# The convolution of a decoder kernel: root and scaling in one piece on VectorE, squares summed on ScalarE

## The chip, the cores and the metric

The kernel runs on one core of one Trainium2 chip. The core has five engines with a queue of instructions each: TensorE (PE in the profile, its weight loads PEld), VectorE (DVE), ScalarE (ACT), GpSimd (POOL) and SyncE (SP, which only issues transfers here). The metric is the device time of one execution in microseconds (us), lower is better; a kernel is run several times and the median counts.

## The reference

A decoder with four blocks of three layers (attention, cross attention, feed-forward), each followed by a residual and a layer norm, on 128 sequences of 64 tokens with 128 features, all in fp32. The change lies in the feed-forward of block L2, a convolution with a small mixture of experts, here cut to what matters:

```python
def _L2_ffn_ref(x, ...):                      # x: 128 x 64 x 128
    xc = conv over the last 3 tokens, each feature by itself + dw_bias
    xc = silu(xc @ pw_w.T + pw_b)
    x1 = x + xc
    logits = x1 @ router_w.T + router_b                      # 8 experts
    top_v, top_i = lax.top_k(logits, 2)
    rw = weights of the two best experts (softmax), zero elsewhere
    ye = silu(einsum('bsd,eod->bseo', x1, expert_w) + expert_b)   # all 8 experts
    combined = einsum('bse,bseo->bso', rw, ye)
    moe_out = combined @ out_w.T + out_b
    a = x1 + moe_out
    h = norm_w * (a / sqrt(mean(a * a) + 1e-6))              # the RMS norm
    ff = gelu(h @ ff_down_w.T + ff_down_b)                   # 128 -> 32
    return h + ff @ ff_up_w.T + ff_up_b
x = layernorm(x + _L2_ffn_ref(x, ...))
```

## The kernel before

The 8192 tokens stay in SBUF as 16 chunks of 512 tokens (`X[c]`, 128 partitions x 4 tiles x 128 features). The convolution, `conv_steps` (L1907 to L2113), takes them in pairs: `turns` is 8, and `pair` is the two chunks of a turn. The work of a turn is written as three parts.

- `begin(i)` (L1943 to L1981) is a generator that prepares turn i: the transposes of X (L1949), the three matmuls of the convolution (L1960), its SiLU on ScalarE (L1962), the sum x1 on GpSimd (L1963), the router's logits (L1968 to L1974) and `top2` on VectorE (L1976, then the helper's L428 to L475, with one tanh on ScalarE, L470). Its result is the table of expert weights `s["w"]`.
- `units(i, n, t)` (L1985 to L2000), eight of them per turn, is the expert work of 128 tokens: matmuls into two PSUM banks (L1992, biases L1994), two SiLU of 512 columns on ScalarE (L1996), the product with the expert weights on VectorE (L1997, 1024 columns), and the sum over the eight experts, its first step on VectorE for even t and on GpSimd for odd t (L1998), the others on GpSimd (L1999, L2000). The units write into a ring of four buffers, and their matmuls into a pool of five PSUM banks.
- `end(i)` (L2002 to L2056) is a generator that finishes turn i: transposes of the experts' sum (L2007) and copies (L2008); the output matmuls (L2016, L2017); on VectorE the biased sum `acc` (L2019); its square on ScalarE (L2021) and the reduction on VectorE (L2022); then the roots; the scaling by root and `norm_w` in eight steps on VectorE (L2033); transposes of the result (L332, copies L339), the residual on GpSimd (L2039, L401), the down and up matmuls (L2044, L2052) with a Gelu between (L2046), and the residual sum (L2054).

`norm` (L2058 to L2067) takes one reciprocal square root for two things at once: the mean squares of turn i and the variances of the layer norm of turn i - 1, whose statistics `ln_stats` computes (L373 to L376). `rsqrt` (L342 to L353) is eleven small dependent instructions on VectorE, on 128 x 16 values: a seed by bit operations (L347, L348) and three Newton steps (L350, L351, L352). `ln_apply` (L379) then writes the layer norm to `X` with a small VectorE step (L382) and four ScalarE instructions per chunk (L385).

The loop at L2083 to L2106 interleaves the three: while the units of turn i are issued one by one, `take` advances the generators of turn i + 1 (`b`), turn i - 1 (`e`) and what is left of turn i - 2 (`tail`). So the order in which the program is traced is set by hand:

```python
elif g == 3:
    take(e, 3)        # acc and squares of both chunks, then norm
elif g == 4:
    take(e)           # the scaling, L2033
...
elif g == 7:
    take(e, 2)        # the transposes of the scaled rows
```

That traced order gives the priority; a scheduler at compile time places each engine's instructions, and takes a later one first where the earlier isn't ready in its model. The order within an engine's queue is fixed after that. `tc.issue_after(ins)` adds an edge: each instruction traced in the block on the engine of `ins` comes behind `ins` in that queue. Before the change no such edge stands inside the loop.

## Time and profile before

| | |
|---|---|
| median of 3 runs | 3176.83 us (3161.66 to 3185.31) |
| profiled execution, own time | 3181.66 us |
| its span | 3179.6 us |
| mean granted TensorE clock | 0.934 |
| busy over the span | PE 88%, PEld 65%, DVE 64%, ACT 51%, POOL 48% |
| expert matmuls of the convolution (L1992) | first at 2125.6 us, last at 2431.2 us |
| one turn of the convolution | 42.2 us from the first L1960 to that of the next turn |
| busy in such a turn | PE 38.5, DVE 35.2, POOL 25.8, ACT 20.9 us |

The profile is one execution as the hardware profiler recorded it. A line of a timeline has the start in us from the span's start, the duration, the engine, the line of the kernel, the operation, the tile written and the tiles read with their shapes, and how many such instructions it merges; in brackets stands the idle time before, with what ended it. A line of the waits has the waiting engine, tile and line, then what it waited for, then the total in us, the number of times and the longest.

### The profile page before, as it was taken

What the parts mean: (1) busy time and instruction counts of PE and PEld (TensorE: products, weight loads), DVE (VectorE), ACT (ScalarE), POOL (GpSimd) and SP (SyncE); (2) the same over time, 40 slices, a digit from 0 to 9 for tenths busy, and PEclk for the clock granted to TensorE, in tenths of its full rate; (3) what the DMA queues carried; (4) which work ended last, traced back from release to release, by engine and by line L of the source; (5) the groups of instructions that cost most, each with busy time, mean ns of one, the idle gap of its engine ahead of it and who ended that gap; (6) DMA issues with size and microseconds to landing.
All of it is one profiled execution on the core that took longest, in us unless ns stands there. A gap on an engine that the chain in (4) does not pass through costs nothing.

```text
span 3179.6 us, 110559 instructions
## 1 busy us (share of the span) xinstructions
PE 2803.0 (88%) x46690; PEld 2051.2 (65%) x46690; DVE 2028.4 (64%) x7310; ACT 1620.5 (51%) x3150; POOL 1516.0 (48%) x1521
## 2 busy tenths in 40 slices
PE   5899979999898899998899989999997679998993
PEld 3789856666666677865577767764433347766882
DVE  3742469667777666553477656667888876674355
ACT  3444468754444465422466555544454556654453
POOL 3566566134555344325277345556665213444244
PEclk9999989999999899889799999989998889997997
DMA  4578921000001100003611000000000000011784
GB/s 128 150 201 261 257 54 43 11 1 3 3 3 44 31 4 4 6 20 98 178 19 18 4 6 4 4 12 1 1 1 7 1 11 18 17 33 49 212 256 120
DMA packets 191633, 182.22 MB, mean 57 GB/s; under 512 B 30176, under 2 KB 166624, under 8 KB 191136
## 3 DMA queue, kind: packets, MB, share of 16 engines
q1 hardware_dynamic: 160688, 136.66, 14.9%
q0 software_dynamic: 20224, 32.28, 4.4%
q8 instruction: 366, 6.00, 0.8%
q10 hardware_dynamic: 10224, 6.22, 0.7%
q14 instruction: 131, 1.07, 0.1%
HBM read 132.34 MB, written 42.73 MB: 55 GB/s over the span
## 4 chain that ended last, share of the span: by engine, by line
PE 55%; DVE 25%; ACT 5%; issue 5%; POOL 5%; DMA 4%; SPq 0%; POOLq 0%; ACTq 0%; DVEq 0%
PE av_ps L1310 9%; DVE m L1243 7%; PE s_ps L1235 6%; PE h_ps L790 5%; PE yg L803 5%; PE t_ps L1273 4%; DMA got<-l_rout,fat 2%; PE ye_ps L1992 2%; PE v_ps L1212 2%; PE xT_ps L332 2%; PE t_ps L1285 2%; POOL x L387 2%; PE y L1134 1%; PE y L1689 1%; DVE lnst L373 1%
## 5 line engine op out<-in xcount | busy, mean ns | idle before, releaser
L1243 DVE TENSOR_REDUCE m<-s_ps 128x8 f32<-128x512 f32 x640 | 397.5, 683 | 122.8 <-PE s_ps L1472 45.4
L1292 ACT ACTIVATE e<-t_ps 128x512 f32<-128x512 f32 x640 | 329.9, 602 | 147.1 <-PE t_ps L1285 146.5
L1310 PE MATMUL av_ps<-vx,e 128*64 128x18 f32 (+1 forms) x10240 | 343.1, 217 | 10.0 <-issue 7.6
L1310 PEld LDWEIGHTS av_ps<-vx,e 128*64 128x64 f32 x10240 | 325.0, 141 | 30.3 <-issue 23.5
L792 ACT ACTIVATE hT<-h_ps,aux 128x256 f32<-128x256 f32 x496 | 206.5, 469 | 218.0 <-PE h_ps L790 105.1
L1273 PE MATMUL t_ps<-eb,kT 32*64 32x128 f32 x10240 | 281.0, 286 | 6.8 <-DVE m L1243 2.4
L1187 POOL TENSOR_SCALAR eb<-qT,small 128x512 f32<-128x512 f32 x75 | 124.1, 1655 | 332.6 <-ACT qT L972 171.2
L825 POOL DMA_INDIRECT got<-l_rout,fat x192 | 193.1, 1006 | 168.0 <-DVE r L835 59.3
L790 PE MATMUL h_ps<-ebT,rw 128*128 128x256 f32 x992 | 241.3, 387 | 13.6 <-DVE ebT L778 8.5
L1273 PEld LDWEIGHTS t_ps<-eb,kT 32*64 32x64 f32 x10240 | 197.9, 132 | 74.0 <-DVE m L1243 25.1
L803 PEld LDWEIGHTS yg<-rw,hT 128*128 128x128 f32 x1984 | 240.7, 192 | 6.3
L803 PE MATMUL yg<-rw,hT 128*128 128x128 f32 x1984 | 241.2, 275 | 0.0
L387 POOL TENSOR_SCALAR x<-xb,lnmv,ln_y 128x128 f32<-128x128 f32 x200 | 157.5, 799 | 169.2 <-DVE ln_y L352 169.1
L1235 PE MATMUL s_ps<-eb,qT 32*64 32x256 f32 x5120 | 220.9, 399 | 10.9 <-DVE m L1243 4.5
L1315 DVE RECIPROCAL rc<-av_ps 128x32 f32<-128x32 f32 (+1 forms) x192 | 61.6, 321 | 241.9 <-PE av_ps L1310 241.8
L765 POOL DMA_INDIRECT aux<-in_x_dram,rat x156 | 160.1, 1026 | 116.3 <-PE h_ps L790 49.1
L790 PEld LDWEIGHTS h_ps<-ebT,rw 128*128 128x128 f32 x992 | 182.0, 194 | 38.4 <-DVE ebT L778 12.9
L804 DVE TENSOR_TENSOR yo<-yg,aux 128x256 f32<-128x256 f32 x124 | 52.3, 422 | 233.4 <-PE yg L803 233.3
L1185 ACT ACTIVATE eb<-qT,small 128x512 f32<-128x512 f32 x160 | 106.9, 715 | 123.6 <-POOL qT L1413 118.9
L1235 PEld LDWEIGHTS s_ps<-eb,qT 32*64 32x64 f32 x5120 | 114.2, 134 | 55.7 <-issue 11.5
L1187 POOL TENSOR_SCALAR eb<-kT,small 128x512 f32<-128x512 f32 x75 | 136.0, 1814 | 24.5 <-ACT kT L972 15.9
L1992 PE MATMUL ye_ps<-w_l2f,box 128*128 128x512 f32 x256 | 135.6, 649 | 0.0
(519 smaller groups left out, 6368.5 us busy)
## 6 DMA issues: line engine op xcount, KB each, us to landing
rw<-in_l0w_dram SPq DMA_DIRECT2D x78, 512.0 KB
rw<-in_l3w_dram SPq DMA_DIRECT2D x46, 512.0 KB
l_rout<-yo SPq DMA_DIRECT2D x124, 128.0 KB
aux<-xd SPq DMA_DIRECT2D x46, 128.0 KB
aux<-in_l0b_dram SPq DMA_DIRECT2D x78, 66.0 KB
xd<-vx SPq DMA_DIRECT2D x5, 1024.0 KB
plan<-xr ACTq DMA_DIRECT2D x18, 256.0 KB
x<-in_x_dram SPq DMA_DIRECT2D x16, 256.0 KB
```

What stands on the lines that cost most here:

```text
L387: (V if on_dve else G).tensor_scalar(X[c][:, t, :], r[:, t, :], mv[:, t, 0:1], y[:, t : t + 1], ALU.subtract, ALU.mult)
L790: s.pe = mm(ps[:, j * GR : (j + 1) * GR], w1[:, (k + j) * P : (k + j + 1) * P], ebT, start=True, stop=True)
L792: s.act_ins = A.activation(hT[k + j], ps[:, j * GR : (j + 1) * GR], s.act, bias=v[:, k + j : k + j + 1])
L803: s.pe = mm(y[:, i * P : (i + 1) * P], hT[k][:, i * P : (i + 1) * P], w2[:, k, :], start=(k == 0), stop=(k == FK - 1))
L825: s.gather = G.indirect_dma_start(out=got[i][k][:, t, :], out_offset=None, in_=s.rout[b][:, :], in_offset=bass.IndirectOffsetOnAxis(ap=at[ ...
L1187: ins = (G if h == 2 and not early else V).tensor_scalar(dst, x, mine, None, ALU.mult)
L1235: mm(ps[g][j * S : (j + 1) * S, u * 256 : (u + 1) * 256].rearrange("p (h k) -> p h k", h=4), rows32(s["q"], g)[:, b], rows32(s["eb"], g)[: ...
L1243: last = V.tensor_reduce(s["m"][:, g, 2 * hf : 2 * hf + 2, :].rearrange("p t h -> p (t h)"), ps[g].rearrange("p (n k) -> p n k", k=S), AX. ...
L1273: mm(ps[g][i * S : (i + 1) * S].rearrange("p (a u j q) -> p a u j q", u=2, a=2, j=2)[:, :, u, j, :], rows32(s["k"], g)[:, b], rows32(s["eb ...
L1292: last = A.activation(e[:, g, :], ps[g], AF.Exp, scale=scale)
L1310: mm(av[j * S : (j + 1) * S, 8 * (u - u0) + n, :], ev[:, n // 2, n % 2, u, j, :], vx[:, 2 * (2 * hf + u) + j, n, :], start=True, stop=True,)
L1992: mm(ps[k].rearrange("p (e d) -> p e d", e=4), s["x1T"][n][:, t * P : (t + 1) * P], w[0][:, 4 * k : 4 * k + 4, :], start=True, stop=False, ...
```

## The change

The root and the scaling of `end(i)` become one step of the generator, right behind the second chunk's sum, and are traced at the slot of unit 3. Each unit traced after that slot, until the next turn's scaling takes its place, is issued with `tc.issue_after(scaled)`, where `scaled` is the last scaling instruction of the turn before; so on VectorE its product and its sum come behind the whole root and scaling. The layer norm's small step and its ScalarE instructions are traced behind the scaling instead of ahead of it. `ln_stats` of a chunk is traced with the sum of that chunk. The slot of unit 4 takes nothing any more; all steps with matmuls keep their slots. The square of a chunk, one ScalarE instruction of 512 columns and a VectorE reduction, becomes four ScalarE instructions of 128 columns that also write their sum (`accum_out`).

```diff
             v = sm.tile([P, 2, 2, TPC], F32, tag="cv", name="cv")
-            acc = []
+            acc, mv = [], []
             for n in pair:
                 ...
                 V.tensor_tensor(h, z.rearrange("p (t d) -> p t d", t=TPC), row("outb")[:, None, :].to_broadcast([P, TPC, D]), ALU.add)
                 sq_ = work("ye", (P, TPC, D), "sq")
-                A.activation(sq_, h, AF.Square)
-                V.tensor_reduce(v[:, 0, n], sq_, AX.X, ALU.add)
+                for t in range(TPC):
+                    A.activation(sq_[:, t, :], h[:, t, :], AF.Square, accum_out=v[:, 0, n, t : t + 1])
                 acc.append(h)
+                if i:
+                    mv.append(ln_stats(S_[i - 1]["r"][n], v[:, 1, n]))
                 yield
             V.tensor_scalar(v[:, 0], v[:, 0], 1.0 / D, 1e-6, ALU.mult, ALU.add)
-
-            y = norm(v, i - 1, S_[i - 1] if i else None)
-            yield
-            hT, base = [], []
+            if not i:
+                G.memset(v[:, 1], 1.0)
+            y = roots(v)
             for n in pair:
                 h = acc[n]
                 for t in range(TPC):
-                    V.scalar_tensor_tensor(h[:, t, :], h[:, t, :], y[:, 0, n, t : t + 1], row("normw"), ALU.mult, ALU.mult)
+                    last = V.scalar_tensor_tensor(h[:, t, :], h[:, t, :], y[:, 0, n, t : t + 1], row("normw"), ALU.mult, ALU.mult)
+            s["scaled"] = last.ins
+            if i:
+                applied(i - 1, mv, y)
             yield
+            hT, base = [], []
             for n in pair:
                 h = acc[n]
                 hT.append(transposed(h, "oT"))
...
-        def norm(v, i, s):
-            ...
+        def roots(v):
+            return rsqrt(v.rearrange("p a n t -> p (a n t)"), 4 * TPC, "rms").rearrange("p (a n t) -> p a n t", a=2, n=2)
+
+        def applied(i, mv, y):
+            for n in pair:
+                ln_apply(2 * i + n, S_[i]["r"][n], mv[n], y[:, 1, n], on_act=True)
...
-        tail = none
+        tail, scaled = none, None
         for i in range(turns):
             ...
             for g in range(8):
-                units(i, g // TPC, g % TPC)
+                with tc.issue_after(scaled) if scaled else nullcontext():
+                    units(i, g // TPC, g % TPC)
                 ...
                 elif g == 3:
                     take(e, 3)
-                elif g == 4:
-                    take(e)
+                    scaled = S_[i - 1]["scaled"] if i else None
                 elif g == 5:
                     take(b)
...
         G.memset(v[:, 0], 1.0)
-        norm(v, turns - 1, S_[turns - 1])
+        mv = [ln_stats(S_[turns - 1]["r"][n], v[:, 1, n]) for n in pair]
+        applied(turns - 1, mv, roots(v))
```

More of the change, by code (lines that the diff above doesn't have):

```diff
@@ L2056, in end @@
             yield
-        def norm(v, i, s):
-            if s is None:
-                G.memset(v[:, 1], 1.0)
-            else:
-                mv = [ln_stats(s["r"][n], v[:, 1, n]) for n in pair]
-            y = rsqrt(v.rearrange("p a n t -> p (a n t)"), 4 * TPC, "rms").rearrange("p (a n t) -> p a n t", a=2, n=2)
-            if s is not None:
-                for n in pair:
-                    ln_apply(2 * i + n, s["r"][n], mv[n], y[:, 1, n], on_act=True)
-            return y
+        def roots(v):
[3 more added lines that the diff above has]
+                ln_apply(2 * i + n, S_[i]["r"][n], mv[n], y[:, 1, n], on_act=True)
         def take(it, n=1):
```

## Prediction

> **What bounds the kernel now.** I began with the page. One execution spans 3179.6 us, its own time is 3181.66 us (2.06 us lie around the span), and the median of the three runs is 3176.83 us, 4.83 us below that execution. The sum below is made on that execution and then shifted by those 4.83 us.
>
> ```profile
> PE 2803.0 (88%) x46690; PEld 2051.2 (65%) x46690; DVE 2028.4 (64%) x7310; ACT 1620.5 (51%) x3150; POOL 1516.0 (48%) x1521
> ```
>
> These shares mix twelve layers. By the source view of L1992 the convolution's expert matmuls run from 2125.6 to 2431.2 us, so whatever the change does must be found in about 355 us, 11% of the span. Inside, the turns repeat: the first L1960 starts at 2250.66, 2292.83, 2335.01 and 2377.17, a period of 42.17 us. The table by stretches for three turns (columns: PE, PEld, DVE, ACT, POOL busy, granted clock, DMA share, GB/s):
>
> ```profile
> 2250.66:2292.83 42.17, 38.95 (x144) 17.68 (x145) 35.24 (x77) 20.85 (x40) 25.85 (x28) 0.92 0.00 1
> 2292.83:2335.01 42.18, 38.54 (x145) 17.27 (x145) 35.20 (x77) 20.86 (x40) 25.84 (x28) 0.92 0.00 0
> 2335.01:2377.17 42.16, 38.53 (x144) 17.53 (x144) 35.24 (x77) 20.85 (x40) 25.84 (x28) 0.92 0.00 1
> ```
>
> PE is nearly full and moves no data to speak of. The view of waits over the same three turns says what PE lacks:
>
> ```profile
> PEld oT_ps L332 <- DVE acc L2033: 15.5, 15, 2.9
> PE oT_ps L332 <- DVE acc L2033: 9.1, 8, 2.1
> PEld u L2052 <- ACT g L2046: 1.7, 2, 1.0
> ```
>
> So one wait matters: the transposes of the scaled rows wait for the scaling. Why that is late is in VectorE's timeline:
>
> ```profile
> 2308.41 0.74 DVE L2025 TENSOR_SCALAR cv<-cv 128x8 f32<-128x8 f32 x1
> 2309.18 0.17 DVE L347 TENSOR_SCALAR rms_b<-cv 128x16 int32<-128x16 int32 x1
> 2309.27 1.22 DVE L1997 TENSOR_TENSOR units<-units,route 128x1024 f32<-128x1024 f32 x1
> ...
> 2312.30 1.24 DVE L351 SCALAR_TENSOR_TENSOR rms_u<-rms_u,cv 128x16 f32<-128x16 f32 x1
> ...
> 2318.66 4.40 DVE L2033 SCALAR_TENSOR_TENSOR acc<-acc,rms_y,rows 128x128 f32<-128x128 f32 x8
> 2322.98 0.21 DVE L436 TENSOR_TENSOR route<-route,t_k 128x64 f32<-128x64 f32 x1
> ```
>
> The root's dozen tiny steps take from 2308.41 to 2317.92, 9.5 us, because products (L1997), sums (L1998) and router steps stand between them.
>
> **Part 1, the root unbroken.** The same steps stand unbroken in the last `end`, where no unit is left: L2025 at 2462.86, the last L352 ending at 2465.34, 2.5 us, then L2033:
>
> ```profile
> 2465.16 0.18 DVE L352 SCALAR_TENSOR_TENSOR rms_y<-rms_u,rms_y 128x16 f32<-128x16 f32 x1
> 2465.52 3.23 DVE L2033 SCALAR_TENSOR_TENSOR acc<-acc,rms_y,rows 128x128 f32<-128x128 f32 x8
> ```
>
> The scaling would end at about 2308.4 + 2.5 + 3.2 to 4.4 = 2314.1 to 2315.3 instead of 2323.1, some 8 us earlier. What PE can take of it: the last L1992 ahead of the transposes ends at 2316.99, the next starts at 2323.12, 6.13 us later; in between lie seven transposes of 0.13 (eight undisturbed ones of L1949 take 1.02) and two L1994 of 0.32, 1.5 us. **4.6 us per turn** is the most that can come back, in six turns (transposes at 2193, 2235, 2277, 2319, 2361 and 2403).
>
> **Part 2, what is late next.** The edges add no instruction; they put the products of units 4 to 7 (4 x 1.14 from start to start) and two sums (2 x 0.60) behind the scaling. Queued behind them on VectorE are the router's steps L1976 to L475; POOL's sums L1998 to L2000 wait for the products, and on POOL's in-order queue L2039 and L401 may stand behind those sums. The chain of waits already shows the router as the next link:
>
> ```profile
> 2281.01 1.14 DVE units L1997
> 2282.15 1.22 DVE route L465
> 2283.37 0.02 issue
> 2283.39 0.23 DVE t_m L428
> 2283.63 0.02 issue
> 2283.65 0.93 DVE route L432
> 2284.58 1.17 DVE t2d L468
> ```
>
> It goes on through the tanh, the SiLU of the next turn's first unit, the table load and the Gelu to L2052 at 2289.01 and L1960 at 2292.83. In the turn of 2292.83, L2052 starts at 2332.00 and the Gelu had ended at 2331.13: only 0.9 us of slack. So what counts is when L468 ends: at 2327.92 now, 19.5 us after L2025 began. After the change the same instructions lie there. Without stalls: root 2.5, scaling 3.2, L382 0.2, products 4.6, sums 1.2, ten router steps at about 0.2 make 13.7 us. To this come waits for POOL. L351 above took 1.24 us instead of 0.17; it ends at 2313.54, and POOL's L1998, which started at 2311.78 for 1.73, ends at 2313.51. Such stretched steps (L351, L350, L352, L382, L2033, L465, L432, L468) add up to about 8 us in this stretch, while POOL ran 11 us. After the change POOL has nothing to sum until the products come, and its 9.9 us (three units' sums 4.8, two L2039 2.6, two L401 2.5) fall on the rest: 4 us of stalls if half hits, 8 us if most does. L468 then ends 17.7 to 21.7 us after L2025, between 1.8 earlier and 2.2 later than now.
>
> So per turn the gain lies between 4.6 (if the SiLU and the Gelu no longer stand behind the tanh on ACT) and -1.3 (if they do and POOL hits: 2.2 less the slack of 0.9). I take **1.0 us**, nearest to the row of the chain: the slack of 0.9 is what PE can win before it meets the second chain, whose own shift I put at nothing. 6 x 1.0 = 6 us.
>
> A row and a rule weighed: the stretched L351 above is one collision. The Trainium skill, "SBUF — State Buffer", section "Who interferes with whom", goes further: every VectorE instruction with two SBUF inputs contends with a GpSimd instruction that reads SBUF, for its whole length. By that rule a turn's POOL work without waits (4 x 1.27 + 8 x 0.73 + 8 x 0.46 + 2 x 1.18 + 2 x 1.31 + 2 x 1.26 = 22.1) and VectorE's two-input work (8 x 1.14 + 4 x 0.60 + 8 x 0.34 + 11 x 0.17 + some 2.2 = 18.3) fill 40.4 of the 42.17 us, an estimate that would cap the gain at 1.8 per turn, 11 us in all, and speaks against the change.
>
> **Part 3, squares on ACT.** Two L2021 (0.63) and two L2022 (0.69) become eight ACT squares of 128 columns with a sum. The page has no such sum. From below: L1827, 128x128, 0.275 each, four make 1.1; from above: L385 at 0.48 each and as much again for the sum, 3.8. Against 0.63 + 0.69 = 1.32 on the path of the second block that is -0.2 to +2.5. I take L385's spacing, 3.19 / 8 = 0.40, four make 1.6: **+0.3 us** per turn, six turns 1.8. VectorE sheds 1.38 us per turn, but in a place where it waits (1.18 and 0.70 us ahead of L2022), so I cost that at nothing; without that cover it would be worth 1.4.
>
> **Part 4, moved steps.** The statistics (L373 to L376) are traced earlier; they ran at 2293 to 2299 already, long before the root: nothing, and 2.8 us if the residual came late. L382 and ACT's eight L385 (3.19 us) go behind the scaling; the oT copies L339 queue behind them, about 2318.5, still before 2321.79 of now: nothing, or 3.2 us if ACT were late. No DMA is touched, and no step of PE, SP or POOL changes its slot.
>
> **Part 5, the last turn.** Here PE stands 6.84 us before the transposes of 2438.94, but VectorE is packed (38.71 us of the 40 from 2400 to 2440), and the second L2007 at 2454.40 waits 4.10 for L2054, which stands behind the next layer's roots. Between 6.84 and a loss of 2.5 I take **4 us**.
>
> **Sum.** -6 + 1.8 - 4 = -8.2 us: 3173.5 on the execution's own time, **3168.6 us** beside the median. I forecast no change that can be told: 1% is about what a measurement of this kernel can tell (31.8 us: below 3145.1 or above 3208.6).
>
> **Rivals.** (A) The forecast, 50%: VectorE with POOL takes over; 3168.6, its own range 3155 to 3185. (B) 20%: PE becomes the only bound, ACT serves the SiLU and the Gelu ahead of the tanh: 6 x 4.6 + 6.84 - 1.8 = 32.6 us, 3144.2. For it: PE's other waits are small; against it: products, router and POOL's sums must still go through VectorE, and 35.2 of 42.17 us are already taken there. (C) 25%, slower: the products held back make POOL's sums and the router late, every tiny router step meets a POOL sum, and PE waits at L2052 and L1992 for ACT behind the tanh: 2.2 from L468 and 2.5 from the squares' upper end, less the slack of 0.9, make 3.8 per turn, six turns and 2.5 at the end: +25, 3202, with 3190 to 3220 around it. It decides once squares and L468 together come more than 0.9 us later than now. For it: the slack of 0.9; against it: VectorE has 2.36 and 0.9 us idle per turn ahead of L1997 and L2054 to absorb it. (D) 5%: the scheduler fills the root's gaps with router steps, and the order of the rest stays: 3176.8.
>
> **How the numbers follow.** Faster by over 1% is half of B (0.10) and a little of A: 0.12. Slower by over 1% is four tenths of C (0.10) and a little of A: 0.12. The rest, 0.76, is within. The low end takes both full gains and the squares' lower end, 27.6 + 6.84 + 1.2 = 35.6 us, 3141, rounded to 3140; the high end, 3206, holds a little over half of C, so that some 2 in 10 lie outside.
>
> **What would show it.** Right: no L1997 between L2025 and the last L2033, which then take 6 to 7.5 us instead of 14.6; the wait at L332 for L2033 falls from 15.5 us in three turns to under 5; the period falls by 0 to 2.5 us; waits at L2052 or L1992 for ACT grow, and L468 ends some 19 us after L2025. Wrong: a period under 39.5 us (B), or over 43.5 (C), or squares above 0.6 us each.

## The result and the profile after

The changed kernel is slower, by a little: a median of 3182.13 us (3166.71 to 3194.1, 20 runs) against 3168.38 us (3149.09 to 3191.43, 20 runs) for the kernel before on the same chip. The ratio is 1.0045, 95% interval 1.0027 to 1.0063. That is far below the 1% of the prediction, and with 20 runs each it is still told from no change: 13.8 us slower, where 8.2 us faster was forecast.

The profiled execution spans 3168.5 us, less than the 3179.6 of before. Single executions scatter by 0.6 to 0.7% to either side, and in these two the stretch ahead of the convolution, which is the same in both programs, differs by 18 us (the first L1992 starts at 2107.7 and at 2125.6). So the traces are compared stage by stage. From the first L1992 to the first instruction of the next layer's scan, the convolution takes 354.7 us before and 362.9 after, 8.2 us more; a second trace of the kernel before, taken later, gives 354.9. The interval of the difference of the medians reaches down to 8.6 us. What the convolution doesn't hold of it, I could not place.

The line numbers after: squares L2022 (L2021 before), mean L2027 (L2025), scaling L2034 (L2033), residual on GpSimd L2044 (L2039), down matmuls L2049 (L2044), Gelu L2051 (L2046), up matmuls "u" L2057 (L2052), residual sum L2059 (L2054). Other steps go by their tiles: oT the transposes of the scaled rows (L332), xT those of X (L1949), sT those of the experts' sum (L2007), pw the convolution's matmuls (L1960), z the output matmuls (L2016, L2017). First the page's line of busy time, then three turns of the changed kernel by stretches, with the same columns as before:

```profile
PE 2768.4 (87%) x46690; PEld 2035.0 (64%) x46690; DVE 2011.8 (63%) x7294; ACT 1630.8 (51%) x3262; POOL 1520.6 (48%) x1521
```

```profile
2234.45:2278.48 44.03, 38.16 (x146) 18.94 (x144) 33.76 (x78) 22.21 (x53) 27.34 (x29) 0.88 0.00 1
2278.48:2322.67 44.19, 38.33 (x146) 18.93 (x144) 33.71 (x74) 22.22 (x53) 26.31 (x29) 0.88 0.00 1
2322.67:2366.91 44.24, 38.39 (x146) 18.93 (x144) 33.55 (x74) 22.21 (x53) 26.23 (x29) 0.88 0.00 1
```

A turn takes 44.2 us instead of 42.2, and the granted clock fell from 0.92 to 0.88. VectorE's timeline shows that the edit does what it says:

```profile
2293.98 0.82 DVE L2027 TENSOR_SCALAR cv<-cv 128x8 f32<-128x8 f32 x1 [1.82 <-ACT sq L2022]
2294.84 0.18 DVE L347 TENSOR_SCALAR rms_b<-cv 128x16 int32<-128x16 int32 x1
...
2296.93 0.17 DVE L352 SCALAR_TENSOR_TENSOR rms_y<-rms_u,rms_y 128x16 f32<-128x16 f32 x1
2297.14 3.21 DVE L2034 SCALAR_TENSOR_TENSOR acc<-acc,rms_y,rows 128x128 f32<-128x128 f32 x8
2300.27 0.22 DVE L382 SCALAR_TENSOR_TENSOR lns<-lnmv,rms_y 128x4 f32<-128x4 f32 x2
2300.42 1.21 DVE L1997 TENSOR_TENSOR units<-units,route 128x1024 f32<-128x1024 f32 x1
```

Mean, root and scaling take 6.4 us (2293.98 to 2300.35) instead of 14.6, with no product in between. The view of waits over the same three turns shows where that went:

```profile
PEld u L2057 <- ACT g L2051: 17.7, 3, 5.9
ACT units L1996 <- POOL box L2000: 17.3, 3, 5.8
PE u L2057 <- ACT g L2051: 16.8, 3, 5.6
...
POOL xb L2044 <- DVE acc L2034: 10.2, 3, 3.4
...
POOL xb L401 <- ACT x L385: 7.5, 3, 2.5
```

The wait at L332 for the scaling (15.5 us) is gone; TensorE now waits 5.6 us a turn at u for the Gelu. Read from below, the lines give the chain of what waited for what. GpSimd has nothing to sum beside the unbroken root (3.4 us idle ahead of L2044), then waits 2.5 us at L401 for ScalarE's L385, which the change put behind the scaling. So the sum of unit 4 ends late. The ring has four buffers, so ScalarE's SiLU of the next turn's unit 0 needs the buffer of unit 4 and waits 5.8 us for GpSimd's L2000; the table load and the Gelu stand behind it in ScalarE's queue.

The clock column by short stretches of the same turn (2309 to the turn's end) shows what comes on top:

```profile
2309.00:2314.00 5.00, 0.00 (x0) 0.00 (x0) 4.76 (x10) 2.65 (x4) 4.92 (x8) 0.81 0.00 0
2314.00:2317.00 3.00, 2.55 (x16) 2.37 (x16) 2.76 (x7) 2.97 (x6) 2.58 (x4) 0.50 0.00 0
2317.00:2320.00 3.00, 3.00 (x9) 1.77 (x9) 2.90 (x5) 1.43 (x3) 0.35 (x1) 0.50 0.00 0
```

After the wait TensorE runs at half clock. The sixteen u products take 2.66 us instead of 1.16. And one more thing moved, though no line of the diff touches it: TensorE's order. Its timeline ahead of pw, of before, then of after:

```profile
2330.08 1.98 PE L1992 MATMUL ye_ps<-w_l2f,box 128*128 128x512 f32 x4
2332.00 1.16 PE L2052 MATMUL u<-w_l2f,g 32*128 32x128 f32 x16
2333.09 0.66 PE L2007 MATMUL sT_ps<-ident,box 128*128 128x128 f32 x4
```

```profile
2314.45 2.66 PE L2057 MATMUL u<-w_l2f,g 32*128 32x128 f32 x16 [5.59 <-ACT g L2051]
2317.04 1.11 PE L2007 MATMUL sT_ps<-ident,box 128*128 128x128 f32 x4
2317.95 1.91 PE L1992 MATMUL ye_ps<-w_l2f,box 128*128 128x512 f32 x2
2319.66 1.06 PE L2007 MATMUL sT_ps<-ident,box 128*128 128x128 f32 x4
2320.51 1.91 PE L1992 MATMUL ye_ps<-w_l2f,box 128*128 128x512 f32 x2
```

Everything from the transposes oT to u now stands one unit earlier in TensorE's queue, presumably because the scheduler's model has the scaling earlier; no run shows that model. The unit that stood ahead of u now stands behind it, so TensorE reaches u with nothing else to do, and pays for that unit later, at half clock (two times 1.91 us instead of 1.98 for all four).

### The profile page after: what moved, and what is told of

It is laid out like the page before. It is cut to its first block, busy times and chain, and to the rows that moved or that the text cites. A ratio compares the mean times of both kernels' runs of the same rounds, so it can differ in the third digit from the quotient of the medians.

```text
span 3168.5 us, 110682 instructions
## 1 busy us (share of the span) xinstructions
PE 2768.4 (87%) x46690; PEld 2035.0 (64%) x46690; DVE 2011.8 (63%) x7294; ACT 1630.8 (51%) x3262; POOL 1520.6 (48%) x1521
## 3 DMA queue, kind: packets, MB, share of 16 engines
q1 hardware_dynamic: 160688, 136.66, 14.9%
## 4 chain that ended last, share of the span: by engine, by line
PE 54%; DVE 22%; POOL 7%; ACT 5%; issue 5%; DMA 5%; SPq 0%; POOLq 0%; ACTq 0%; DVEq 0%
PE av_ps L1310 9%; DVE m L1243 7%; PE s_ps L1235 6%; PE h_ps L790 5%; PE yg L803 5%; PE t_ps L1273 4%; DMA got<-l_rout,fat 2%; PE ye_ps L1992 2%; POOL x L387 2%; PE v_ps L1212 2%; PE xT_ps L332 2%; PE t_ps L1285 2%; PE y L1134 1%; PE y L1689 1%; DVE lnst L373 1%
## 5 line engine op out<-in xcount | busy, mean ns | idle before, releaser
L1310 PEld LDWEIGHTS av_ps<-vx,e 128*64 128x64 f32 x10240 | 319.2, 139 | 32.4 <-issue 25.1
L790 PEld LDWEIGHTS h_ps<-ebT,rw 128*128 128x128 f32 x992 | 181.9, 193 | 40.1 <-DVE ebT L778 13.2
L1992 PE MATMUL ye_ps<-w_l2f,box 128*128 128x512 f32 x256 | 135.9, 648 | 0.0
```

What stands on the lines that cost most here:

```text
L790: s.pe = mm(ps[:, j * GR : (j + 1) * GR], w1[:, (k + j) * P : (k + j + 1) * P], ebT, start=True, stop=True)
L1310: mm(av[j * S : (j + 1) * S, 8 * (u - u0) + n, :], ev[:, n // 2, n % 2, u, j, :], vx[:, 2 * (2 * hf + u) + j, n, :], start=True, stop=True,)
L1992: mm(ps[k].rearrange("p (e d) -> p e d", e=4), s["x1T"][n][:, t * P : (t + 1) * P], w[0][:, 4 * k : 4 * k + 4, :], start=True, stop=False, ...
```

## The experiments

All ratios are against the kernel before, on the same chip and in the same rounds (the chips differ: the kernel before took 3277 us beside the first four experiments, 3293 us beside e16 to e18, and 3164 to 3168 us beside the others). A turn's time is taken between the first L1960 of two turns.

### First: which part of the change costs (e1 to e4)

**e1_edges_only**: the changed kernel with the old squares.

```diff
-                for t in range(TPC):
-                    A.activation(sq_[:, t, :], h[:, t, :], AF.Square, accum_out=v[:, 0, n, t : t + 1])
+                A.activation(sq_, h, AF.Square)
+                V.tensor_reduce(v[:, 0, n], sq_, AX.X, ALU.add)
```

> The changed kernel with the squares put back as before (one 512-column square and a VectorE reduction per chunk); edges and merged step stay. Theory (the held-back products make the sums of unit 4 late on GpSimd, the next turn's first SiLU waits for that ring buffer, the Gelu stands behind it on ScalarE, and PE waits at the up matmul for the Gelu): the squares have no part in it, the period from one turn's first convolution matmul to the next stays at 44.0 us (43.7 to 44.4), PE still waits some 5.6 us per turn at the up matmul, time 0.2 to 0.6% above the kernel before. Rival 1 (the squares with their eight accumulator reads cost the time): the period falls back to 42.2 to 42.6 and the time to that of the kernel before.

Measured: 1.0059 (1.0032 to 1.0086), turns of 44.2 to 44.3 us after the first, and the same two waits. **e2_squares_only** is the complement: the kernel before with the new squares (the same lines, the other way round).

> The kernel before with only the squares summed by ScalarE. Theory: the second chunk's root starts at most 0.2 us earlier or later, the period stays at 42.0 to 42.4 us, no difference in time beyond 0.2%. Rival 1 (squares): the period rises to 43.5 or more, and the time by 0.3 to 0.5%.

Measured: 1.0007 (0.9981 to 1.0032). The turns are uneven (40.6 to 44.2 us); two of the three long ones have 10 us at half clock instead of 7. The theory's 42.0 to 42.4 us a turn was missed: the middle turns of this trace average 43.3 us, close to the rival's 43.5. In the time the squares neither cost nor win anything that can be told, and in the changed kernel itself the old squares (e1) made the turn no shorter.

**e3_no_edges** keeps all of the change but the edges:

```diff
-                with tc.issue_after(scaled) if scaled else nullcontext():
-                    units(i, g // TPC, g % TPC)
+                units(i, g // TPC, g % TPC)
```

> The changed kernel without the edges on the units: root and scaling are still one step of the generator at the slot of unit 3, the squares are summed by ScalarE. Theory: products stand again between the root's steps, unit 4's sum is early, no SiLU waits for a ring buffer; the period is 41.8 to 42.6 us and the time within 0.3% of the kernel before. Rival 2 (the moved step and the moved layer norm, not the edges, cost the time): the period stays at 44 us.

Measured: 1.0007 (0.9979 to 1.0035); the SiLU no longer waits for GpSimd, and the wait at L332 is back. The turns are 42.1 to 45.4 us after the first, two of four longer than the forecast. In the same rounds the edges without the squares gave 1.0059 (e1), so the loss in time comes with the edges. **e4_sums_first** attacks the chain on GpSimd by putting its residual steps behind the units' sums:

```diff
-                b = with_bias(2 * i + n, "upb")
-                G.tensor_tensor(b, b, h, ALU.add)
+                with tc.issue_after(S_[i + 1]["summed"]) if i + 1 < turns else nullcontext():
+                    b = with_bias(2 * i + n, "upb")
+                    G.tensor_tensor(b, b, h, ALU.add)
```

> The changed kernel, with GpSimd's residual steps of a turn (bias and residual, then the scaled rows) queued behind the sums of the units traced ahead of them, by one edge each on GpSimd. Theory: unit 4's and 5's sums no longer stand behind two residual steps and behind the layer norm that frees their buffer; the SiLU's wait for the ring falls from 5.8 to under 3 us per turn and PE's wait at the up matmul from 5.6 to under 3; the period falls to 41 to 42.5 us, time 0.0 to 0.4% below the changed kernel's, unless the residual steps become the late ones. Rival 3 (VectorE and GpSimd together are full, whatever the order): the period stays within 0.5 us of 44.

Measured: 1.0018 (0.9989 to 1.0047). The wait at u fell only to 3.4 us a turn, a new one of the same size stood at the transposes of the sums, and every turn took 43.8 us. My number for the turn was missed, and the third rival's (within 0.5 us of 44) was met:

```profile
PE u L2058 <- ACT g L2052: 10.1, 3, 3.4
PE sT_ps L2007 <- DVE xb L2060: 8.8, 3, 3.3
```

### Second: take single links out of the chain (e5 to e8)

**e5_ring5** adds a fifth buffer to the ring.

```diff
-            y = ring[count[0] % 4]
+            y = ring[count[0] % 5]
...
+        ring.append(work("tab", (P, E8, D), "fifth"))
```

> The changed kernel with a fifth buffer in the ring of SiLU results; nothing else differs. Theory (late sums of unit 4 hold the ring's buffer, so ScalarE's SiLU of the next turn's unit 0 waits 5.8 us a turn for GpSimd, and the table load, the Gelu and TensorE's u stand behind it in ScalarE's order): the SiLU of unit 0 now needs the buffer of unit 3, whose sums end ahead of the root, so the wait ACT units <- POOL box L2000 at that place (17.3 us in three turns) is under 3 us, TensorE's wait at L2057 for the Gelu falls from 16.8 us in three turns to under 5, and a turn takes 40.5 to 42.5 us instead of 44.1; the time is 0.2 to 0.4% below the changed kernel's, so 0.998 to 1.002 of the kernel before. Rival (VectorE and GpSimd are full together: what GpSimd loses beside the unbroken root is not made up, whoever waits for it): the wait turns up at another buffer or at the residual, and a turn stays at 43.5 to 44.2 us, ratio 1.004 to 1.006. Second rival (the Gelu needs the residual's GpSimd step): L2057 finds its Gelu but VectorE's L2059 waits for GpSimd's L2044, turn 42.5 to 43.5.

Measured: 1.0036 (1.0008 to 1.0064), turns of 43.7, 42.4 and 43.3 us. The SiLU and the Gelu come early as the theory said, and the theory falls all the same, for TensorE waits at the very same place for something else, the copy that stands behind the tanh, so for the router on VectorE:

```profile
ACT t2d L470 <- DVE t2d L468: 15.4, 3, 5.1
...
PE u L2057 <- ACT xp L1952: 14.6, 3, 4.9
```

**e6_apply_first** puts the layer norm's apply ahead of the scaling again, inside the edges.

```diff
             y = roots(v)
+            if i:
+                applied(i - 1, mv, y)
             for n in pair:
...
-            if i:
-                applied(i - 1, mv, y)
```

> The changed kernel with the layer norm's apply (L382 and L385) put ahead of the convolution's scaling again; the edges stay. Theory (the moved step frees the residual's buffer late: GpSimd's L401 waits 2.5 us a turn for ScalarE's L385 and the units' sums stand behind it): the wait POOL xb L401 <- ACT x L385 (7.5 us in three turns) is gone or under 2 us, the scaling ends some 1 us later, the sums of unit 4 end 1 to 2.5 us earlier, TensorE's wait at L2057 for the Gelu falls from 16.8 us in three turns to 9 to 13, a turn takes 42.3 to 43.5 us instead of 44.1, ratio 1.001 to 1.004 of the kernel before. Rival (VectorE and GpSimd are full together): a turn stays at 43.5 to 44.2, ratio 1.004 to 1.006, and the 2.5 us come back as another wait of GpSimd. Second rival (the step's place costs all of the loss): the turn is back at 42.2, ratio 0.999 to 1.001.

Measured: 1.0045 (1.0022 to 1.0067). L401's wait is gone, the wait at u is 2.5 us a turn, and a new one of 3.4 us stands at the transposes xT, for VectorE's L1976. A turn takes 44.4 us: nearest to the first rival. **e7_gelu_first** issues the SiLU of unit 0 behind the Gelu.

```diff
+                gelu = S_[i - 2]["gelu"] if i > 1 else None
                 with tc.issue_after(scaled) if scaled else nullcontext():
-                    units(i, g // TPC, g % TPC)
+                    with tc.issue_after(gelu) if gelu else nullcontext():
+                        units(i, g // TPC, g % TPC)
+                if g == 0:
+                    take(tail)
```

> The changed kernel with the SiLU of the next turn's unit 0 issued behind the Gelu on ScalarE, so that the Gelu no longer stands behind the SiLU that waits for GpSimd; the sums stay as late as they are. Theory: TensorE's wait at L2057 for the Gelu goes from 16.8 us in three turns to under 4, the Gelu comes some 5 us earlier, but the SiLU of unit 0 then comes behind the Gelu, another table load and the tanh, so TensorE's unit 1 or 2 waits for a bank instead: a turn takes 41.5 to 43.5 us, ratio 1.000 to 1.004 of the kernel before. Rival (VectorE and GpSimd are full together): the Gelu is early, VectorE's L2059 and the next unit's products come no earlier, and a turn stays at 43.5 to 44.2 us, ratio 1.004 to 1.006. Second rival (the Gelu's own place is all of the loss): turn 40 to 41.5, ratio 0.996 to 0.999.

Measured: 1.0058 (1.0032 to 1.0084), turns of 45.4 to 46.2 us, worse than both. The Gelu is early, and u's second half then waits 7.0 us a turn for VectorE's L2059. **e8_before** is a second trace of the kernel before, with no edit.

> The kernel before, unchanged, for its stage times on this chip. All theories: turns of 41 to 42.6 us each, the convolution from its first product to the first scan 354 to 358 us, no wait of ScalarE's SiLU for GpSimd at the turn's unit 0, TensorE waiting 13 to 16 us in three turns at the transposes L332.

Measured: turns of 42.2 to 42.5 us (the first 39.8), 354.9 us for the convolution.

Four single links taken out (e4 to e7), four times a wait came back elsewhere, and each time the new wait led to VectorE. That needs another reading. Between the mean L2027 and the residual sums L2059, VectorE has a fixed list: mean, root, scaling, the layer norm's two L382, five products, three sums, the router's eighteen small steps, two residual sums. This is its end in the changed kernel:

```profile
2316.85 0.20 DVE L475 TENSOR_SCALAR route<-route 128x64 f32<-128x64 f32 x1
2317.14 1.23 DVE L1997 TENSOR_TENSOR units<-units,route 128x1024 f32<-128x1024 f32 x1
2318.29 0.68 DVE L2059 TENSOR_TENSOR xb<-u,xb 128x512 f32<-128x512 f32 x1
2318.89 0.68 DVE L1998 TENSOR_TENSOR units<-units 128x512 f32<-128x512 f32 x1
2319.49 0.68 DVE L2059 TENSOR_TENSOR xb<-u,xb 128x512 f32<-128x512 f32 x1
```

So I cut each turn in two in the trace: the list, from the start of L2027 to the end of the second L2059 (2293.98 to 2320.17 here, 26.2 us; before 2308.41 to 2334.55, 26.1), and TensorE's stretch, from there to the next L2027. The list frees the PSUM banks of u, which the second transposes of the sums or pw take next. In the stretch TensorE runs pw, two or three units and z without a stop, and VectorE waits for it. Means of the three middle turns, in us; "busy" is VectorE's busy time inside the list, "half" the time of the stretch at half clock by the clock records:

| kernel | list | busy | stretch | half | turn |
|---|---|---|---|---|---|
| before | 25.8 | 24.7 | 16.4 | 0.0 | 42.2 |
| changed | 26.2 | 25.2 | 18.0 | 2.1 | 44.2 |
| e1_edges_only | 26.1 | 25.1 | 18.2 | 2.4 | 44.3 |
| e2_squares_only | 26.2 | 25.4 | 17.1 | 1.2 | 43.3 |
| e4_sums_first | 26.4 | 25.4 | 17.7 | 3.2 | 44.1 |
| e5_ring5 | 26.2 | 25.2 | 16.9 | 0.8 | 43.1 |
| e6_apply_first | 27.6 | 26.6 | 16.8 | 0.4 | 44.4 |
| e7_gelu_first | 26.6 | 25.3 | 19.1 | 3.6 | 45.7 |
| e9_late_hold | 25.4 | 24.7 | 18.6 | 5.2 | 43.9 |
| e10_root_edges | 26.1 | 25.1 | 16.1 | 1.3 | 42.2 |
| e11_ring5_router | 26.2 | 25.3 | 18.4 | 3.1 | 44.7 |
| e14_full | 26.2 | 25.3 | 15.3 | 3.4 | 41.6 |
| e15_late_hold_pw | 25.3 | 24.7 | 15.4 | 0.0 | 40.7 |

(From L2027 to L2027, so a turn may differ from the text's by some tenths. In e3, e12, e13 and e16 to e18 the residual sums come later, 27 to 31 us after the mean, as u comes later or more stands ahead of them; list and stretch then shift against each other, and VectorE is 93 to 97% busy inside the list, in e3 87%. A trace is one execution and the ratio is of many: e9's turns in the table are longer than before and its time is not. So the table shows where a turn's time lies, the ratio what the program takes.)

The scaling ends between 5.4 and 14.9 us after L2027 in these kernels; the list ends 25.3 to 26.6 us after it in all but e6 (27.6). **VectorE is 95 to 98% busy inside the list, so its order decides who waits, not when it ends.** Busy time counts a stretched step in full. At short durations (the tenth percentile of each line in the trace) the list's 50 instructions add up to some 18 us, before and after, an estimate; 6 us or more of it is steps that take longer, part of it beside GpSimd's work like the L351 of the prediction's timeline. So what is full would be VectorE together with GpSimd, as the rivals of these experiments have it. No run took work out of the list; that it bounds the turn is read from these orders.

### Third: other orders of the list (e9 to e11)

**e9_late_hold** holds back only units 6 and 7.

```diff
                     take(e, 3)
-                    scaled = S_[i - 1]["scaled"] if i else None
...
                 elif g == 5:
                     take(b)
+                    scaled = S_[i - 1]["scaled"] if i else None
```

> The changed kernel with the edges on the products of units 6 and 7 alone; those of units 4 and 5 stand inside the root again, with four small steps of the router, and the scaling follows the root at once. Theory (the four products held back to behind the scaling make GpSimd idle beside the root and then late, with the units' sums, the ring and the router behind it): the sums of units 4 and 5 run beside the root again, ScalarE's SiLU of unit 0 waits under 1 us for GpSimd, TensorE's wait at the u for the Gelu is under 4 us in three turns, the scaling ends 11 to 13 us behind the start of L2027 (14.6 in the kernel before, 7.3 in the changed one), so the waits of TensorE at L332 lie between 3 and 10 us in three turns (15.5 before, none in the changed kernel); a turn takes 40.0 to 41.9 us, ratio 0.996 to 0.9995 of the kernel before. Rival (any hold on products costs more than the earlier scaling gives, as VectorE and GpSimd are full together): a turn of 42.2 to 43.5, ratio 1.000 to 1.004.

Measured: 0.9989 (0.9961 to 1.0017). All its waits are as expected, and the turn isn't: 40.1, 41.7, 42.3, 43.6 and 44.4 us, growing. Here is TensorE's timeline at the beginning of the last of these turns and at its end, and then the clock column of the same places; pw takes 5.42 us in the kernel before:

```profile
2326.14 7.96 PE L1960 MATMUL pw_ps<-xp,ctab 128*128 128x512 f32 x12
...
2366.41 0.39 PE L1994 MATMUL ye_ps<-ctab 32*128 32x512 bf16 x1
2368.98 1.12 PE L2007 MATMUL sT_ps<-ident,box 128*128 128x128 f32 x4 [2.18 <-DVE xb L2059]
```

```profile
2326.14:2334.00 7.86, 7.86 (x14) 3.38 (x14) 5.14 (x20) 1.14 (x3) 4.77 (x5) 0.67 0.00 0
...
2369.00:2374.00 5.00, 5.00 (x9) 2.30 (x10) 4.78 (x11) 1.57 (x3) 3.50 (x5) 0.50 0.00 0
```

A wait of 2.2 us for VectorE's list, and the clock is at half behind it, in the stretch where TensorE is the bound. From turn to turn more of the slow time falls into the stretch: with 3.4 us of half clock in it the stretch takes 17.6 us, with 6.2 us it takes 19.1, so 0.54 us for each.

**e10_root_edges** holds the products back only to the end of the root (`scaled` is then the root's last instruction).

```diff
-            s["scaled"] = last.ins
+            s["scaled"] = FIRST["root"]
```

> The changed kernel with the edges of the four products on the last instruction of the root instead of the last of the scaling: one product then stands between the root and the scaling and one sum inside VectorE's work behind it, and GpSimd takes unit 4's sum between its two residual steps. Theory: unit 4's sums end 3 to 5 us earlier, so the SiLU of unit 0 waits 5.8 - 4 = 1 to 3 us a turn for GpSimd instead of 5.8, TensorE waits 2 to 4 us at u for what is late next (the tanh, whose root of the router stays behind the products), a turn takes 42.5 to 43.8 us, ratio 1.001 to 1.004. Rival (the hold beside the root alone, GpSimd's idle 3.4 us, is all of the loss): unchanged against the changed kernel, 43.8 to 44.3, ratio 1.004 to 1.006.

Measured: 1.003 (1.0002 to 1.0058), turns of 42.1 to 43.1 us after the first, a wait of 2.7 us a turn at u for the copy behind the tanh, which is late as with the fifth buffer. So far as the theory said; but the SiLU's wait for GpSimd is gone altogether, where 1 to 3 us were forecast. **e11_ring5_router** has the fifth buffer, and puts the products of units 4 to 6 behind the router's difference.

```diff
-        V.tensor_tensor(d, m1, m2, ALU.subtract)
+        FIRST["t2d"] = V.tensor_tensor(d, m1, m2, ALU.subtract).ins
...
                 elif g == 6:
                     take(b)
+                    with tc.issue_after(scaled) if scaled else nullcontext():
+                        with tc.issue_after(FIRST["t2d"]) if held else nullcontext():
+                            for p in held:      # the products and sums of units 4 to 6
+                                p()
```

> The changed kernel with the fifth ring buffer, and in the five middle turns the products of units 4 to 6 behind the router's difference L468 too, so that the scaling is followed by the router's ten small steps in one piece. Theory (with the fifth buffer the Gelu is early and the tanh with the two L1952 copies behind it is what TensorE's second half of u waits for, 4.9 us a turn): the tanh comes right behind the layer norm's activations, some 10 us earlier, TensorE's wait at u falls from 14.6 us in three turns to under 5, and a turn takes 40.5 to 42.5 us, ratio 0.997 to 1.002. Rival (VectorE and GpSimd full together): the units' sums end later instead, TensorE waits at the transposes L2007 of the sums, turn 43 to 44, ratio 1.003 to 1.006.

Measured: 1.0049 (1.0022 to 1.0075), turns of 44.6 to 46.2 us after the first. The tanh comes 10 us earlier, no wait at u is left, and TensorE waits 7.9 us at the transposes of the sums for the end of the list. The rival's wait and ratio, with turns longer than its 43 to 44 us:

```profile
PE sT_ps L2009 <- DVE xb L2061: 23.6, 3, 7.9
```

### Fourth: the wait, the clock, and TensorE's order (e12 to e18)

**e12_warm** fills the wait at u with ten products that nobody reads.

```diff
             A.activation(g, ps[:64, :], AF.Gelu, bias=col("downb")[:64])
+            if i < turns - 1:
+                spare.append([wide("ye_ps") for _ in range(2)])    # unit 1's banks
+                for _ in range(10):
+                    mm(spare[0][0].rearrange("p (e d) -> p e d", e=4), ident, w[0][:, :4, :], start=True, stop=True)
```

> The changed kernel with ten TensorE products a turn that nobody reads (ident by expert weights, 128x512, about 0.43 us each, into the PSUM bank that unit 1 overwrites afterwards), issued ahead of the transposes xT, so in the 5.6 us in which TensorE waits for the Gelu. Nothing is saved; only TensorE is not idle. Theory A (the loss is the wait and also the half clock that follows it): the profile's clock rows show under 4 us a turn at half clock between the Gelu and the next turn instead of 10.2, the sixteen u products take 1.2 us instead of 2.7, and a turn takes 41 to 43 us instead of 44.1, ratio 0.999 to 1.003 of the kernel before. Theory B (the wait alone counts, the clock only shows it): the wait is filled, a turn stays at 43.8 to 44.8, ratio 1.004 to 1.007.

Measured: 1.0017 (0.999 to 1.0044). I had mis-sized them: each takes two passes of 0.43 us, 8.6 us in all, so u starts 2.9 us behind its Gelu. The clock stays full, and a turn with 8.6 us of useless work is 1.1 us shorter than the changed kernel's (stretch columns as above):

```profile
2267.12:2310.23 43.11, 42.80 (x166) 20.08 (x164) 34.13 (x75) 22.24 (x53) 25.38 (x28) 1.00 0.00 1
```

This trace also prices what follows u. From the start of u to pw TensorE needs 3.0 to 3.8 us before, 7.7 to 8.3 us after and, with the clock full, 4.3 us here (four middle turns each): so 3.5 to 4 us of what the changed kernel loses behind u are the half clock, and the rest, 0.5 to 1.3 us, would be the unit that now stands there.

**e16_warm6** has six instead, 5.2 us.

> e12_warm with six idle products a turn instead of ten: 6 x 0.86 = 5.2 us of TensorE's time in the 5.6 us in which it waits for the Gelu. In e12 the ten took 8.6 us, u began 2.7 us behind its Gelu, and no stretch of the convolution was at half clock. Theory A (half clock behind the wait is a large part of the loss): u begins within 0.3 us of its Gelu, the clock stays full, and a turn takes 43.1 - 2.65 = 40.5 us (40.0 to 41.2), 3.7 us less than the changed kernel's though nothing waits less; ratio 0.995 to 0.999 of the kernel before. Theory B (the wait alone counts): a turn of 43 to 44.2, ratio 1.002 to 1.006.

Measured: 1.0035 (1.0008 to 1.0063), a turn of 45.1 us. Theory A misses by over 4 us. The wait at u is gone (0.4 us), the next one stands 2.2 us at the transposes of the sums for VectorE's L2059, and 2.3 us of half clock follow in the stretch. The list, too, ends later (27.6 us after the mean instead of 26.2). My reading is that an idle TensorE ahead of the list's end costs nothing by itself and that half clock in the stretch does; this run alone doesn't show it. **e17_warm_before** fills the wait at the transposes oT in the kernel before with three such products.

```diff
+        def idle(ps):
+            for _ in range(3):
+                mm(ps.rearrange("p (e d) -> p e d", e=4), ident, w[0][:, :4, :], start=True, stop=True)
...
-                hT.append(transposed(h, "oT"))
+                hT.append(transposed(h, "oT", fill=idle if n == pair[0] and 0 < i < turns - 1 else None))
```

> The kernel before with three idle products a turn (2.6 us) ahead of the first transposes oT, in the five middle turns, where TensorE waits 2.1 us and more for the scaling. The order of some other steps of TensorE moves with them (the transposes oT come in one piece). Theory A: half clock falls from 6.8 us a turn to 0 to 3.4, a turn takes 39.8 to 41.5 us instead of 42.2, ratio 0.995 to 0.999: the kernel before loses to the half clock too, and the change with its wait filled (e16) is ahead by no more than 1.5 us a turn. Theory B (the wait is what counts): 42.0 to 43.5, ratio 0.999 to 1.003.

Measured: 1.0036 (1.0014 to 1.0058), a turn of 43.0 us. Its half clock stayed, mostly, at 6.8 us a turn. So it doesn't show what a full clock would give; in the kernel before all of the half clock lies inside the list, and the stretch has none.

**e13_ring5_units** has the fifth buffer, and unit 2's products ahead of u again.

```diff
-                elif g == 1:
-                    take(tail)
-                    take(e, 2)
                 elif g == 2:
+                    with tc.issue_after(S_[i]["mm"].ins):      # unit 2's last matmul
+                        take(tail)
+                    take(e, 2)
                     take(b, 2)
```

> The changed kernel with the fifth ring buffer, and with TensorE's u put behind the products of the next turn's unit 2 (2.3 us of work that stood behind u); the transposes of the sums follow u as before. Theory (TensorE's unchanged order has nothing to do while it waits for the tanh): of the 4.9 us wait at u (with the fifth buffer) 2.3 us are filled, the half clock falls from 7 to 10 us a turn to 7 or less, a turn takes 40.5 to 42.3 us instead of 43.1, ratio 0.997 to 1.001. Rival (VectorE and GpSimd are full, TensorE only waits for them elsewhere): the wait moves to the transposes of the sums or to the next products, a turn of 43 to 44, ratio 1.003 to 1.006.

Measured: 1.0038 (1.002 to 1.0056), turns of 42.4 to 44.9 us: the wait at u shrank from 4.9 to 3.1 us and a new one of up to 2.2 us stood at pw. The rival, more or less.

The last idea follows from the table: if the list is fixed, move TensorE's work out of the stretch and beside the list. **e14_full** is e11 with the transposes of the sums behind pw.

```diff
                 elif g == 1:
                     take(tail)
-                    take(e, 2)
                 elif g == 2:
                     take(b, 2)
+                    with tc.issue_after(S_[i + 1]["pw"].ins) if i + 1 < turns else nullcontext():
+                        take(e, 2)
```

> The changed kernel with the fifth ring buffer, the router's small steps ahead of the held products as in e11_ring5_router, and TensorE's transposes of the units' sums (L2007 of the changed kernel) put behind unit 2 and the depthwise products pw, which need only the early tanh and its copies. Theory (TensorE's order decides): the 7.9 us a turn that TensorE waited at those transposes in e11 are filled by 7.7 us of unit 2 and pw, half clock at 0 to 4 us a turn, a turn takes 38.5 to 40.8 us, ratio 0.993 to 0.998 of the kernel before: a kernel that beats both. Rival (VectorE and GpSimd are full): the wait turns up at z, at pw or at the next root, a turn of 42 to 44.9, ratio 1.000 to 1.006.

Measured: 0.9971 (0.9949 to 0.9993), the convolution 348.6 us, 6.1 less than before. From mean to mean the turns take 38.8, three times 41.0 and 42.7 us, mostly longer than forecast: TensorE now waits 4.1 us a turn at pw for VectorE's L2061, one of the places that the rival named. **e15_late_hold_pw** is e9 with its second transposes of the sums behind the first half of pw.

```diff
                     take(tail)
-                    take(e, 2)
+                    take(e)
                 elif g == 2:
-                    take(b, 2)
+                    take(b)
+                    with tc.issue_after(S_[i + 1]["pw"].ins) if i + 1 < turns else nullcontext():
+                        take(e)
+                    take(b)
```

> e9_late_hold (edges on units 6 and 7 alone) with TensorE's second transposes of the sums put behind the first three depthwise products pw. In e9 TensorE waited 2.2 us a turn there for GpSimd and VectorE, and the clock rows show the products behind it at half clock; the turn grew from 40.1 to 44.4 us as that stretch moved into pw. Theory (wait and half clock decide): that wait is filled, half clock at 0 to 3.4 us a turn, all five turns at 39 to 41 us, ratio 0.994 to 0.998: faster than both kernels. Rival (VectorE and GpSimd are full): a turn of 42 to 44, ratio 0.999 to 1.002 as in e9.

Measured: 0.997 (0.9945 to 0.9994). The turns hold at 40.7 us, the first at 38.7 with the clock full throughout, and the convolution takes 346.8 us, 7.9 less than before:

```profile
2245.90:2286.63 40.73, 37.03 (x145) 16.98 (x145) 33.29 (x75) 22.45 (x54) 24.96 (x29) 0.96 0.00 1
2286.63:2327.36 40.73, 37.13 (x145) 16.93 (x145) 33.29 (x75) 22.26 (x54) 24.98 (x29) 0.96 0.00 1
```

Both kernels are faster than the one before and than the changed one, as their theories expected, at the upper end of their ratios. **e18_hold_pw_warm** tried to fill e15's wait at oT with two idle products (the edit of e17 with two).

> e15_late_hold_pw with two idle products a turn (1.7 us) ahead of the first transposes oT, where TensorE still waited 2.8 us a turn and the clock fell to half for 3.4 us. Theory A: the half clock is gone, a turn takes 39.0 to 40.3 us instead of 40.7, ratio 0.993 to 0.9975 of the kernel before. Theory B: the products cost what they take, a turn of 40.7 to 42.5, ratio 0.997 to 1.001.

Measured: 1.005 (1.0028 to 1.0072), turns of 45.8 to 46.9 us. They moved the scheduler's order of TensorE, the Gelu came 3.4 us later, and TensorE waited 4.4 us a turn for it, at half clock after that. Worse than either theory.

## Why the prediction was wrong

**Part 1 held.** The scaling ends 8.3 us earlier, counted from the mean, where 8 were forecast, and the transposes L332 lost their wait.

**Part 3 held.** One square of 0.63 and a reduction of 0.69 on the second chunk's path (from the end of L2019 to the mean 1.9 us) became four pairs of 0.29 and 0.19 us with a step of 0.29 (1.8 us to the mean): nothing, where +0.3 was taken. The time of e2 (1.0007) agrees; the longer turns of its single trace don't, and stay open.

**Part 2 is the step that failed**, and with it the sum's -6 us. It took 1.0 us a turn as won, between +4.6 and -1.3; the turn lost 2.0, outside these bounds. The step that failed is the one from TensorE's wait to the turn: what TensorE won at u ("the slack of 0.9", with the second chain's shift at nothing) was taken as won for the whole turn. Counted from the mean, that chain was indeed no later: L468 ends at 19.7 us instead of 19.5, the Gelu at 20.4 instead of 22.7 or more, and u starts at 20.5 instead of 22.8 to 23.6. TensorE waits 5.6 us there because it is ready sooner, 14.9 us after the mean. Then u and the unit that now stands behind it run at half clock, and pw starts 28.2 to 28.8 us after the mean instead of 26.6 to 27.0.

Part 2 also looked for the one chain that is late next and named the router and the tanh. In the changed kernel the chain ahead of u was another: GpSimd's sums, the ring's four buffers, the SiLU ahead of the Gelu. That alone would be a wrong name. e5 shows more: with that chain out of the way, the router's chain stands right behind, and behind it (e7, e9, e11) the residual sum. They are late together, since all are on one VectorE list of 25 to 26 us that was full before and is full after. I had worked out that the steps would still take 17.7 to 21.7 us up to L468 (19.7 measured), so that L468 would on the whole come no earlier; I then let TensorE win the slack of 0.9 us, when neither the list nor the stretch behind it had become shorter. (GpSimd ran 14.5 us beside those steps before, by the profile, not the 11 that I read; the bounds held all the same.)

The page named in the prediction, the Trainium skill's "SBUF — State Buffer" with "Who interferes with whom", spoke against the change, and rightly so in its direction: VectorE's and GpSimd's work between them left little room. The measured bound is narrower than the estimate made from it: VectorE is some 96% busy, stretched steps included, not over the turn, but over the list.

**Part 4 failed in two places that were costed at nothing.** L385 behind the scaling frees the residual's buffer late: GpSimd's L401 waits 2.5 us for it. e6 took that wait away and won nothing, so this didn't decide. And "no step of PE changes its slot" holds for the traced order only: in TensorE's queue oT to u moved one unit ahead. Of the 2.0 us a turn, the list has 0.4 and the stretch 1.6. With 0.54 us for each us of half clock (e9), the 2.1 us of it in the stretch make 1.1, an estimate; the other 0.5 would be the unit that now stands behind u. The 4.3 us of e12 from u to pw speak for both parts. No run put that unit back by itself; e13 did so together with the fifth buffer, and another wait came.

**Part 5 failed.** The last turn gave nothing (from its pw to the scan 103.6 us, 103.1 before and 104.7 in e8). Its wait of 6.8 us at the transposes became 5.1 there and 4.9 at the down matmuls, and the 4.1 at L2007 became 6.3.

**The rivals.** C had the sign and its first clause, GpSimd's sums late; its 3.8 us a turn from the squares and the tanh was not what happened. B saw rightly that ScalarE would serve the SiLU and the Gelu ahead of the tanh, and nothing came of it. The test "a period over 43.5 us" decided against the forecast.

## What to carry to other kernels

When a wait goes away, add up what the engine behind it still has to do before the loop closes: if that list is full, as here, its order only chooses who waits, and the gain must come from moving the other engine's work beside it (e15). An edge on VectorE moved TensorE's order here, so compare each engine's order, not only the edited one. Idle time of TensorE has a second price, the clock behind it, and in these runs it was paid where TensorE was the bound.

## What the runs showed of the hardware

A wait of 2.2 us was enough to halve TensorE's clock (e9: pw 7.96 us instead of 5.42), and in e15 one of 1.6 us. The Trainium skill, "TensorE: Matmul & The Clock Gate", section "Part 1: The HAM clock gate", has the clock fall after an idle window of about 3.4 us; here the slow time does come in pieces of 3.41 us (6.8 us a turn before, 10.2 in the changed kernel, in the clock records), but shorter waits start it, in some turns and not in others.

Where the half clock fell beside VectorE's list (6.8 us a turn in the kernel before) the list ended 25.8 us after the mean, against 25.3 with half as much of it (e15), so there it cost little; in the stretch it cost 0.54 us per us (e9). And small two-input steps of VectorE were stretched beside GpSimd's work: after the change L432 took 1.34 us while GpSimd's L401 ran (2311.66 to 2312.92) and L471 1.17 us while L1998 ran (2314.09 to 2315.40), where L433 took 0.21 us in a gap between GpSimd's steps (2313.55).
